# Attention over a paged cache: the products of a sequence's own values, for two sequences at once, as 64-row products in the two halves of the array

## The chip, the core and the metric

The kernel runs on one core of a Trainium2 chip. The metric is the device time of one execution in microseconds (us), as the median of several runs. The profile is one further execution, recorded by the hardware profiler. Its engines are TensorE (PE, with its weight loads listed apart as PEld), VectorE (DVE), ScalarE (ACT), GpSimd (POOL) and SyncE (SP).

## The reference, cut to what matters

Four residual layers are chained over x of 64 sequences x 32 tokens x 512 features, all in float32. The change touches only the third, an attention with a paged key-value cache:

```python
q = einsum('bsd,ed->bse', x, Wq).reshape(64, 32, 32, 128)      # 32 query heads
k = einsum('bsd,ed->bse', x, Wk).reshape(64, 32, 8, 128)       # 8 key heads
v = einsum('bsd,ed->bse', x, Wv).reshape(64, 32, 8, 128)
q, k = rope(rmsnorm(q)), rope(rmsnorm(k))
k_all = concatenate([k_cache[block_table], k], axis=1)         # 512 cached + 32 own keys
v_all = concatenate([v_cache[block_table], v], axis=1)
probs = softmax(where(valid, einsum('bqhd,bkhd->bhqk', q, k_all) * SCALE, -1e30))
o = einsum('bhqk,bkhd->bqhd', probs, v_all)
y = einsum('bse,de->bsd', o.reshape(64, 32, 4096), Wo)
```

Four query heads share one key head. For a sequence and a key head, the output is a sum over 512 cached values and over the sequence's own 32 values. The change concerns the second part.

## The kernel before, in words

The attention stage takes the 8 key heads in two halves of 4 (HKP = 4), and in each half the 16 tiles of 128 tokens (4 sequences of 32 tokens). That makes 32 steps. A step has 16 turns: 4 sequences b times 4 key heads g. The 128 rows of a turn are 4 query heads x 32 tokens.

The order on TensorE is written by hand: every matmul goes through `on_pe`, which chains it to the one before. A turn issues (loop from L831): `turned` (four 128x128 transposes of the turn's probabilities into `prT_ps`), a slot list, `start(i + 2)` (the scores of two turns ahead, two matmuls into `sc`), a second slot list, and `values` (four matmuls: 512 cached values against the turned probabilities, into `po`). The slot lists hold the projections of the next step (`pv`, `pk`, `pq`), the output product of the step before (`py`) and the transposes of the rotated queries and keys (`qkT_ps`). The order on the other engines is left to a scheduler that works when the program is built.

In the last turn of a sequence (g = 3) `own_turned` (L681) transposes the sequence's own probabilities. The result `own_prT` has 128 rows: 4 key heads x 32 own keys. `own_values` (L535) lays the own values out as `own_vt`, 128 rows x 4 slots x 128: the 32 rows of key head g are filled in slot g alone, and everything else is zero. So `own_part` (L696) can contract over all 128 rows for each g, in four 128x128x128 matmuls that add to the four groups of `po`, after which one DVE copy moves `po` (128x512, one PSUM bank) to `oT`. There are two `po` buffers, used by turns, and two each of `own_pr` and `own_vt`; `own_prT` has one.

In a float32 program each matmul stands in the trace as two passes, each with its own weight load, so the 4 matmuls are 8 records. A transpose is one record.

The evacuation, as it stands before:

```python
po = pos.pop(b)
for g in range(HKP):
    part(po[:, g, :], [(own_vts[b % 2][:, g, :], own_prT)], False, g == HKP - 1)
nc.vector.tensor_copy(oT[:, :, b % SEQ * S:(b % SEQ + 1) * S],
                      po.rearrange("p g (h s) -> p (g h) s", h=REP))
```

The first layer of the same kernel, which the change does not touch, multiplies 32 tokens of each of 4 sequences with weights of their own: at L183 four matmuls have 32 output partitions each and write the four quarters of one bank's partitions. The trace calls these `py<-w,xT 128*32`. The prediction reads them.

Of the kernel before, what the change touches and what calls it, by code (L numbers as in the profile page):

```python
# [24 lines left out]
F32 = mybir.dt.float32  # L25
# [8 lines left out]
P = 128  # L34
B, S, D = 64, 32, 512
NT = B * S // P
SEQ = P // S
# [6 lines left out]
HQ, HK, HD = 32, 8, 128  # L44
# [3 lines left out]
HKP = HK // HALVES  # L48
HQP = HQ // HALVES
REP = HQ // HK  # L50
# [410 lines left out]
def attention(c, known, x_in, y_part, y_out, tail):  # L461
# [10 lines left out]
    tc, nc, a = c.tc, c.nc, c.a  # L472
    half = HD // 2
    n_c = L // P
    with ExitStack() as outer:
        wvk = outer.enter_context(tc.tile_pool(name="l2_key_value_weights", bufs=1))
        xp = outer.enter_context(tc.tile_pool(name="l2_x", bufs=1))
        wk = outer.enter_context(tc.tile_pool(name="l2_work", bufs=1))
        kp = outer.enter_context(tc.tile_pool(name="l2_fixed", bufs=1))
# [5 lines left out]
        ps = ctx.enter_context(tc.tile_pool(name="l2_psum", bufs=1, space=PSUM))  # L485
# [8 lines left out]
        prs = [kp.tile([P, NK], F32, name=f"pr{i}") for i in range(3)]  # L494
        own_prs = [kp.tile([P, HKP * S], F32, name=f"own_pr{i}") for i in range(2)]
        vts = [kp.tile([P, n_c, HKP * HD], F32, name=f"vt{i}") for i in range(2)]
        own_vts = [kp.tile([P, HKP, HD], F32, name=f"own_vt{i}") for i in range(2)]
        for t in own_vts:
            nc.gpsimd.memset(t, 0.0)

        def transposes(tag, name, pieces):
            pt = ps.tile([P, len(pieces), P], F32, tag=tag, name=name)
            for m, piece in enumerate(pieces):
                c.on_pe(nc.tensor.transpose(pt[:, m, :], piece, c.ident))  # L504
            return pt

        def part(out, pairs, first, last):
            for i, (lhsT, rhs) in enumerate(pairs):
                c.on_pe(nc.tensor.matmul(out, lhsT, rhs, start=first and i == 0,  # L509
                                         stop=last and i == len(pairs) - 1))  # L510
# [24 lines left out]
        def own_values(b, v):  # L535
            j = b % SEQ
            for g in range(HKP):
                nc.vector.tensor_copy(own_vts[b % 2][g * S:(g + 1) * S, g, :],
                                      v[j * S:(j + 1) * S, g * HD:(g + 1) * HD])


# [138 lines left out]

        def own_turned(b):  # L681
            pt = transposes("tq", "own_prT_ps", [own_prs[b % 2]])
            own_prT = wk.tile([P, P], F32, name="own_prT")
            nc.scalar.copy(own_prT, pt[:, 0, :])
            return own_prT

        pos = {}

        def values(b, g, prT):

            if g == 0:
                pos[b] = ps.tile([P, HKP, P], F32, tag="po", bufs=2, name="po")
            part(pos[b][:, g, :], [(vts[b % 2][:, n, g * HD:(g + 1) * HD], prT[:, n, :])
                                   for n in range(n_c)], g == 0, False)

        def own_part(b, own_prT, oT):  # L696

            po = pos.pop(b)
            for g in range(HKP):
                part(po[:, g, :], [(own_vts[b % 2][:, g, :], own_prT)], False, g == HKP - 1)  # L700
            nc.vector.tensor_copy(oT[:, :, b % SEQ * S:(b % SEQ + 1) * S],  # L701
                                  po.rearrange("p g (h s) -> p (g h) s", h=REP))

        def weights(h, what):

# [46 lines left out]
        oTs, stores = {0: qp.tile([P, HQP, P], F32, name="oT")}, []  # L752
        p = projections[0]
# [36 lines left out]
        for s, (h, T) in enumerate(steps):  # L790
            if s:
                oTs[s] = qp.tile([P, HQP, P], F32, name="oT")
            slots = [[] for _ in range(2 * per)]
            if s == 0:
                slots[0].append(partial(projections[0].turned, 2))
                slots[2].append(partial(projections[0].turned, 3))
                slots[2].append(partial(own_keys, 0, 1, projections[0].kT))
            if s + 1 < len(steps):
                p = projections[s + 1]
                for what, at in zip(("v", "k") + GROUPS,  # L800
                                    ((1, 2), (3, 4), (6, 7), (8, 10), (11, 13), (14, 16))):
                    for u in range(2):
                        slots[at[u]].append(partial(p.product, what, u))
                for what, at in zip(("k",) + GROUPS, (9, 12, 15, 17, 20)):
                    slots[at].append(partial(p.turned, what))
            else:
                slots[16].append(tail.scaled)
                for m, at in enumerate((20, 22, 24, 26)):
                    slots[at].append(partial(tail.fold, ps, m))
            if s + 2 < len(steps):  # L810
                slots[18].append(projections[s + 2].load)
                slots[24].append(projections[s + 2].tables)
                slots[28].append(projections[s + 2].x)
                if steps[s + 2][0] != h:

                    for what, at in zip(("v", "k") + GROUPS, (3, 5, 8, 11, 14, 17)):
                        slots[at].append(partial(weights, steps[s + 2][0], what))
            if s + 2 == len(steps):
                for at, f in zip((17, 20, 23, 26, 29), tail.weights(wp, wvk)):
                    slots[at].append(f)  # L820
            if s:
                out = Output(*steps[s - 1], oTs.pop(s - 1), ws)
                for u, at in enumerate((18, 19, 21, 23, 25, 27, 29, 31)):
                    slots[at].append(partial(out.product, u))
                if steps[s - 1][0] != h:
# [357 lines left out]
```

## Time and profile before

| what | value |
|---|---|
| median of 3 runs (range) | 3809.74 us (3806.65 to 3811.78) |
| time of the profiled execution | 3798.88 us |
| span of the profiled execution | 3797.0 us |
| mean granted TensorE clock | 0.997 |
| PE / DVE / ACT / POOL busy | 3732.0 / 1797.3 / 1299.0 / 1284.4 us |
| attention stage, about 1173 to 3626 us of the span | PE busy 2446.5 of 2453.0 us |
| records of the own values' products on PE | 1024, 275 ns each |

The span runs from the first to the last instruction; the profiled execution took 1.9 us more than its span, and lies 10.9 us below the median of the runs. "Busy" is the union of the records of an engine, so matmuls that overlap are counted once. A record of a matmul reaches from its start to the end of its way through the array; records that follow each other overlap, so the spacing of their starts is what one costs the engine.

### The profile page before, as it was taken

What the parts mean: (1) busy time and instruction counts of PE and PEld (TensorE: products, weight loads), DVE (VectorE), ACT (ScalarE), POOL (GpSimd) and SP (SyncE); (2) the same over time, 40 slices, a digit from 0 to 9 for tenths busy, and PEclk for the clock granted to TensorE, in tenths of its full rate; (3) what the DMA queues carried; (4) which work ended last, traced back from release to release, by engine and by line L of the source; (5) the groups of instructions that cost most, each with busy time, mean ns of one, the idle gap of its engine ahead of it and who ended that gap; (6) DMA issues with size and microseconds to landing.
All of it is one profiled execution on the core that took longest, in us unless ns stands there. A gap on an engine that the chain in (4) does not pass through costs nothing.

```text
span 3797.0 us, 60480 instructions
## 1 busy us (share of the span) xinstructions
PE 3732.0 (98%) x17992; PEld 2629.6 (69%) x17992; DVE 1797.3 (47%) x4863; ACT 1299.0 (34%) x3008; POOL 1284.4 (34%) x1289
## 2 busy tenths in 40 slices
PE   6999999999999999999999999999999999999999
PEld 2444788888886777777777777777777777777755
DVE  5443111111116566555655565556555665556433
ACT  0111111111114444444444444444444444444411
POOL 0112100000006454444444444444444554444222
PEclk9999999999999999999999999999999999999999
DMA  5104211111115433444334346454444444444522
GB/s 191 34 26 165 89 42 42 42 42 45 35 55 164 130 115 115 118 120 117 114 117 122 115 155 197 145 151 119 118 121 125 118 118 121 122 123 117 156 69 62
DMA packets 402036, 407.45 MB, mean 107 GB/s; under 512 B 48592, under 2 KB 312784, under 8 KB 401712
## 3 DMA queue, kind: packets, MB, share of 16 engines
q1 hardware_dynamic: 352560, 241.68, 20.9%
q0 software_dynamic: 46848, 157.72, 13.7%
q10 hardware_dynamic: 2304, 4.20, 0.3%
q8 instruction: 147, 2.41, 0.3%
q14 instruction: 177, 1.45, 0.1%
HBM read 382.44 MB, written 20.97 MB: 106 GB/s over the span
## 4 chain that ended last, share of the span: by engine, by line
PE 94%; DVE 1%; issue 1%; ACT 1%; SPq 1%; DVEq 1%; DMA 1%; POOL 1%; POOLq 0%; ACTq 0%
PE po L509 15%; PE sc L660 12%; PE py L509 12%; PE pq L509 11%; PE prT_ps L504 6%; PE pg L122 5%; PE pu L122 5%; PE pz L122 4%; PE po L958 3%; PE ph L122 3%; PE pv L509 3%; PE pk L509 3%; PE pd L228 2%; PE qkT_ps L504 2%; PE pt L122 2%; PE py L183 1%
## 5 line engine op out<-in xcount | busy, mean ns | idle before, releaser
L531 POOL DMA_INDIRECT vt<-in_v_rows,v_rows x512 | 499.4, 975 | 823.7 <-PE po L509 727.7
L509 PEld LDWEIGHTS po<-prT,vt 128*128 128x128 f32 x4096 | 530.5, 192 | 183.1 <-issue 177.5
L665 DVE CUSTOM_DVE_ANT_0 pr<-sc,mask 128x544 f32<-128x544 f32 x512 | 369.1, 721 | 434.5 <-PE sc L660 433.9
L660 PE MATMUL sc<-kt,qT 128*128 128x288 f32 (+1 forms) x2048 | 556.1, 394 | 7.3 <-DMA kt<-in_kT 4.1
L667 ACT ACTIVATE pr<-pr,low 128x544 f32<-128x544 f32 x512 | 383.2, 748 | 501.9 <-DVE low L665 499.8
L509 PE MATMUL po<-prT,vt 128*128 128x128 f32 x4096 | 541.7, 275 | 0.0
L660 PEld LDWEIGHTS sc<-kt,qT 128*128 128x128 f32 x2048 | 369.4, 191 | 183.9 <-issue 108.7
L509 PE MATMUL py<-wo,oT 128*128 128x512 f32 x1024 | 480.2, 592 | 0.8 <-DVE oT L701 0.8
L509 PE MATMUL pq<-wq,xT 128*128 128x512 f32 x1024 | 480.7, 593 | 0.0
L678 ACT COPY prT<-prT_ps 128x512 f32<-128x512 f32 x512 | 299.4, 585 | 417.5 <-PE prT_ps L504 413.3
L672 DVE TENSOR_SCALAR pr<-pr,low 128x512 f32<-128x512 f32 x512 | 312.6, 611 | 16.7
L504 PE MATMUL prT_ps<-ident,pr 128*128 128x128 f32 x2048 | 307.7, 273 | 0.3 <-DVE pr L672 0.3
L509 PEld LDWEIGHTS py<-wo,oT 128*128 128x128 f32 x1024 | 191.9, 190 | 137.9 <-issue 125.8
L509 PEld LDWEIGHTS pq<-wq,xT 128*128 128x128 f32 x1024 | 182.4, 190 | 130.1 <-issue 125.3
L669 DVE RECIPROCAL low<-low 128x1 f32<-128x1 f32 x512 | 83.1, 162 | 347.8 <-ACT pr L667 346.7
L504 PEld LDWEIGHTS prT_ps<-ident,pr 128*128 128x128 f32 x2048 | 241.4, 142 | 0.4 <-issue 0.4
L126 POOL TENSOR_TENSOR rs<-rs,minus_half 128x4 f32<-128x4 f32 x160 | 166.4, 1040 | 196.3 <-DVE rs L547 195.1
L563 POOL TENSOR_TENSOR rot<-rot,swapped 128x512 f32<-128x512 f32 x160 | 202.8, 1267 | 1.0
L670 ACT ACTIVATE own_pr<-pr,low 128x32 f32<-128x32 f32 x512 | 164.1, 321 | 113.4 <-DVE low L669 113.4
L546 DVE TENSOR_REDUCE rs<-squares 128x4 f32<-128x512 f32 x160 | 109.6, 685 | 168.4 <-ACT squares L544 164.4
L564 POOL TENSOR_TENSOR rot<-rot,rs 128x512 f32<-128x512 f32 x160 | 177.7, 1110 | 8.0
L122 PE MATMUL pg<-xT,gate1T 128*128 128x256 f32 (+1 forms) x704 | 170.2, 382 | 0.8 <-DVE sg L334 0.8
(217 smaller groups left out, 4815.4 us busy)
## 6 DMA issues: line engine op xcount, KB each, us to landing
kt<-in_kT SPq DMA_DIRECT2D x2048, 64.0 KB
xt<-x SPq DMA_DIRECT2D x48, 256.0 KB
wq<-in_WqT SPq DMA_DIRECT2D x12, 1024.0 KB
sets<-in_cond0T SPq DMA_DIRECT2D x4, 2048.0 KB
vt<-in_v_rows,v_rows POOLq DMA_INDIRECT x512, 3.7
wo<-in_WoT SPq DMA_DIRECT2D x8, 1024.0 KB
y<-y SPq DMA_DIRECT2D x32, 256.0 KB
xT<-in_xT SPq DMA_DIRECT2D x4, 1024.0 KB
```

Of the source, the lines that this page charges most:

```text
L122: self.nc.tensor.matmul(out, lhsT, rhs, start=i == 0, stop=i == len(pairs) - 1)
L126: self.nc.gpsimd.tensor_tensor(t, t, self.minus_half[:, :n], ALU.pow)
L504: c.on_pe(nc.tensor.transpose(pt[:, m, :], piece, c.ident))
L509: c.on_pe(nc.tensor.matmul(out, lhsT, rhs, start=first and i == 0, stop=last and i == len(pairs) - 1))
L531: nc.gpsimd.indirect_dma_start(out=vts[b % 2][:, n, :], out_offset=None, in_=a["v_rows"], in_offset=bass.IndirectOffsetOnAxis(ap=rows[h][: ...
L563: nc.gpsimd.tensor_tensor(r, r, tmp, ALU.add)
L564: last = nc.gpsimd.tensor_tensor(r, r, rs.unsqueeze(2).to_broadcast([P, REP, HD]), ALU.mult)
L660: c.on_pe(nc.tensor.matmul(sc[:, lo + n * PSIZE:lo + m * PSIZE].rearrange("p (n k) -> p n k", k=PSIZE), q, kt[:, n:m, g, :], start=True, s ...
L665: nc.vector.tensor_tensor_reduce(pr[:, :NK], sc[:, lo:lo + NK], masks[h, b], -SCALE, 3.0e38, ALU.add, ALU.min, low[:, 0:1])
L667: nc.scalar.activation(pr[:, :NK], pr[:, :NK], AF.Exp, bias=low[:, 0:1], scale=-1.0, accum_out=low[:, 1:2])
L672: nc.vector.tensor_scalar(pr[:, :L], pr[:, :L], low[:, 2:3], None, ALU.mult)
L678: nc.scalar.copy(prT, pt)
```

## The change

The own values of two sequences (even b, then odd b) are multiplied together, after the odd one's last turn. `own_vt` shrinks to 2 slots: the rows of key heads 0 and 1 (rows 0 to 63) use slots 0 and 1, and so do those of key heads 2 and 3 (rows 64 to 127). A product is now taken over 64 rows. It is placed in the upper or the lower half of the array's rows, and the two halves write different PSUM banks: `po0` collects key heads 0 and 1 of both sequences, `po1` key heads 2 and 3. Each bank therefore lives through two sequences, and there is one buffer of each where there were two of `po`. The 8 own products of the two sequences are issued alternating between the halves. `own_prT` has two buffers, as the even sequence's is kept until the odd one's is there. Two DVE copies, one for each bank, move the results of both sequences. The own values of both sequences are laid out by calls in turns 0 and 2 of the even sequence, where each sequence's were laid out in the first turn of the sequence before it.

```diff
-        own_vts = [kp.tile([P, HKP, HD], F32, name=f"own_vt{i}") for i in range(2)]
+        own_vts = [kp.tile([P, 2, HD], F32, name=f"own_vt{i}") for i in range(2)]
...
-                nc.vector.tensor_copy(own_vts[b % 2][g * S:(g + 1) * S, g, :],
+                nc.vector.tensor_copy(own_vts[b % 2][g * S:(g + 1) * S, g % 2, :],
                                       v[j * S:(j + 1) * S, g * HD:(g + 1) * HD])
...
-            own_prT = wk.tile([P, P], F32, name="own_prT")
+            own_prT = wk.tile([P, P], F32, name="own_prT", bufs=2)
...
-            if g == 0:
-                pos[b] = ps.tile([P, HKP, P], F32, tag="po", bufs=2, name="po")
-            part(pos[b][:, g, :], [(vts[b % 2][:, n, g * HD:(g + 1) * HD], prT[:, n, :])
-                                   for n in range(n_c)], g == 0, False)
+            if b % 2 == 0 and g == 0:
+                pos[:] = [ps.tile([P, 2, 2, P], F32, tag=f"po{n}", name="po") for n in range(2)]
+            part(pos[g // 2][:, b % 2, g % 2, :], [(vts[b % 2][:, n, g * HD:(g + 1) * HD], prT[:, n, :])
+                                                   for n in range(n_c)], b % 2 == 0 and g % 2 == 0, False)
...
-        def own_part(b, own_prT, oT):
-            po = pos.pop(b)
-            for g in range(HKP):
-                part(po[:, g, :], [(own_vts[b % 2][:, g, :], own_prT)], False, g == HKP - 1)
-            nc.vector.tensor_copy(oT[:, :, b % SEQ * S:(b % SEQ + 1) * S],
-                                  po.rearrange("p g (h s) -> p (g h) s", h=REP))
+        def own_part(b, own_prTs, oT):
+            for u in range(2):
+                for g in range(2):
+                    for n in range(2):
+                        q = slice(n * P // 2, (n + 1) * P // 2)
+                        part(pos[n][:, u, g, :], [(own_vts[u][q, g, :], own_prTs[u][q, :])],
+                             False, u == g == 1)
+            at = (b - 1) % SEQ * S
+            for n in range(2):
+                nc.vector.tensor_copy(
+                    oT[:, 2 * n * REP:2 * (n + 1) * REP, at:at + 2 * S]
+                    .rearrange("p m (u s) -> p m u s", u=2),
+                    pos[n].rearrange("p u g (h s) -> p (g h) u s", h=REP))
...
                 if g == HKP - 1:
-                    own_prT = own_turned(b)
+                    own_prTs = ([] if b % 2 == 0 else own_prTs) + [own_turned(b)]
...
-                if g == HKP - 1:
-                    own_part(b, own_prT, oTs[s])
-                elif g == 0 and i:
-                    own_values_of(i + HKP)
+                if b % 2 and g == HKP - 1:
+                    own_part(b, own_prTs, oTs[s])
+                elif b % 2 == 0 and g in (0, 2) and i >= HKP:
+                    own_values_of(i - g + g // 2 * HKP)
```

More of the change, by code (lines that the diff above doesn't have):

```diff
@@ L682, in own_turned @@
             pt = transposes("tq", "own_prT_ps", [own_prs[b % 2]])
-            own_prT = wk.tile([P, P], F32, name="own_prT")
+            own_prT = wk.tile([P, P], F32, name="own_prT", bufs=2)
             nc.scalar.copy(own_prT, pt[:, 0, :])
             return own_prT
-        pos = {}
+        pos = []
         def values(b, g, prT):
-            if g == 0:
-                pos[b] = ps.tile([P, HKP, P], F32, tag="po", bufs=2, name="po")
-            part(pos[b][:, g, :], [(vts[b % 2][:, n, g * HD:(g + 1) * HD], prT[:, n, :])
-                                   for n in range(n_c)], g == 0, False)
-        def own_part(b, own_prT, oT):
-            po = pos.pop(b)
-            for g in range(HKP):
-                part(po[:, g, :], [(own_vts[b % 2][:, g, :], own_prT)], False, g == HKP - 1)
-            nc.vector.tensor_copy(oT[:, :, b % SEQ * S:(b % SEQ + 1) * S],
-                                  po.rearrange("p g (h s) -> p (g h) s", h=REP))
+            if b % 2 == 0 and g == 0:
[15 more added lines that the diff above has]
+                    pos[n].rearrange("p u g (h s) -> p (g h) u s", h=REP))
         def weights(h, what):
```

## The prediction

> **What bounds the kernel now.** I read the page first, then the groups of instructions by shape, the waits of TensorE inside the attention stage, and the timeline around the own products and around the first layer's narrow matmuls.
>
> ```profile
> span 3797.0 us, 60480 instructions
> PE 3732.0 (98%) x17992; PEld 2629.6 (69%) x17992; DVE 1797.3 (47%) x4863; ACT 1299.0 (34%) x3008; POOL 1284.4 (34%) x1289
> ...
> PEclk9999999999999999999999999999999999999999
> ...
> PE 94%; DVE 1%; issue 1%; ACT 1%; SPq 1%; DVEq 1%; DMA 1%; POOL 1%; POOLq 0%; ACTq 0%
> PE po L509 15%; PE sc L660 12%; PE py L509 12%; PE pq L509 11%; PE prT_ps L504 6%; PE pg L122 5%; PE pu L122 5%; PE pz L122 4%; PE po L958 3%; PE ph L122 3%; PE pv L509 3%; PE pk L509 3%; PE pd L228 2%; PE qkT_ps L504 2%; PE pt L122 2%; PE py L183 1%
> ```
>
> TensorE is busy 98% of the span at full clock, and 94% of the chain that ended last lies on it. The waits of PE between 1200 and 3610 us are these, in total us, times and the longest:
>
> ```profile
> PE sc L660 <- DMA kt<-in_kT: 4.1, 3, 3.0
> PE sc L660 <- DVE low L665: 0.8, 1, 0.8
> PE qkT_ps L504 <- POOL rot L564: 0.6, 1, 0.6
> PE prT_ps L504 <- DVE pr L672: 0.3, 1, 0.3
> ```
>
> That is 5.8 us in 2410. So PE time taken out of this stage comes out of the end, and new PE time goes onto it, until another engine is late. DVE is 47% busy. These are the groups the change touches:
>
> ```profile
> L538 DVE COPY own_vt<-v 32x128 f32<-32x128 f32 x512 | 137.5, 269 | 51.8 <-PE po L509 42.2 <-issue 2.3
> L509 PE MATMUL po<-own_prT,own_vt 128*128 128x128 f32 x1024 | 135.3, 275 | 0.0
> ...
> L701 DVE COPY oT<-po 128x512 f32<-128x512 f32 x128 | 87.8, 686 | 3.1 <-PE po L509 2.3
> ```
>
> The 135.3 us is the union of records with their tails. The cost is the spacing of starts, which the timeline shows (start, duration, engine, count):
>
> ```profile
> 2411.06 0.97 PEld L509 LDWEIGHTS po<-own_prT,own_vt 128*128 128x128 f32 x8
> ...
> 2411.17 1.06 PE L509 MATMUL po<-own_prT,own_vt 128*128 128x128 f32 x8
> ...
> 2412.06 0.60 PE L504 MATMUL prT_ps<-ident,pr 128*128 128x128 f32 x4
> ```
>
> From 2411.17 to 2412.06, 8 passes take 0.89 us: 0.112 us each, the loads at the same spacing hidden behind them. Two sequences cost 1.79 us, all 64 pairs 114 us.
>
> **The change: what the products cost.** There are 8 products of 64 rows for a pair, so still 16 passes and 16 loads; only running two at once can gain. No row of the trace has 64x128 products. The nearest is L183, where four matmuls use quarters of the array's columns:
>
> ```profile
> 80.38 3.70 PE L122 MATMUL ph<-yT,up 128*128 128x512 f32 x8
> ...
> 84.01 0.16 PEld L183 LDWEIGHTS py<-w,xT 128*32 128x32 f32 x8 [0.76 <-issue]
> ...
> 84.01 1.92 PE L183 MATMUL py<-w,xT 128*32 128x512 f32 x16
> 85.87 3.70 PE L122 MATMUL ph<-yT,up 128*128 128x512 f32 x8
> ```
>
> A full-array pass of 512 columns starts every 0.43 us. Sixteen one after another would take 6.9 us; these took 1.92, so four run at once. The two passes of each matmul do not prevent it.
>
> From 80.38 to 85.87 are 5.49 us; 8 full passes and 4 quartets at 0.428 make 5.14. So going into the split array and back costs 0.35 us: each time the array runs empty and the next load lies open. Here the load on the way in has 32 columns. Ours has 128, and the load rows below say 192 against 111 ns, 0.08 more: **0.43 us for a pair's two switches**.
>
> If two halves run at once, a pair takes 8 slots of 0.112, 0.89 us, plus 0.43: 1.32 against 1.79, saving 0.46, times 64 **29.6 us**.
>
> **Two rules of the Trainium skill, against the rows.** The section "LDWEIGHTS (loading the stationary operand)" of "TensorE: Matmul & The Clock Gate" speaks against the change: a load's time follows its columns, not its rows.
>
> ```profile
> L509 PEld LDWEIGHTS po<-own_prT,own_vt 128*128 128x128 f32 x1024 | 124.6, 192 | 0.0
> ...
> L183 PEld LDWEIGHTS py<-w,xT 128*32 128x32 f32 x512 | 20.8, 111 | 73.3 <-DVE w L179 41.9 <-issue 29.0 <-DVE coeffs L878 0.8
> ...
> L122 PEld LDWEIGHTS pz<-actT,down1T 96*128 96x128 f32 x64 | 12.2, 191 | 1.7
> ```
>
> The trace agrees: 96 rows load in 191 ns as 128 do in 192. Halving the rows shortens no load, and loads already come every 0.112 us. If they pass one by one, 16 take 1.79 us, and the sum becomes plus 0.43 x 64 = 27.5 us. Against that stands the load row at 84.01: eight loads of 111 ns each within 0.16 us. By the slope (81 ns for 96 columns) 32 columns take 0.027 us, so eight in a row would end at 0.30. Loads into different parts of the array do overlap, at least when the parts are columns. The section "Key Properties" of "TensorEngine Tiling (Array Packing)" says it for parts in general, and also that a change of mode drains the array, by an amount it doesn't name; the 0.35 us is that amount here. No run yet shows row halves. Ends: minus 29.6 and plus 27.5. I take the first, since the nearest row shows both matmuls and loads at once.
>
> **What is moved and who could be late.** The order of instructions in the changed kernel leaves PE as it was but for these products; ACT, POOL and SP keep their instructions, the vt and kt DMAs among them, so no queue is passed. `own_prT`'s second buffer is copied turns earlier; the odd one's copy (271 ns on ACT) stands ahead of its products as before, so it costs nothing.
>
> The new wait: each bank has one buffer, so the next pair's first `values` waits for po0's copy on DVE. The built order puts six `own_vt` copies ahead of the two oT copies, and these wait for the pair's products. The same place before, at a step's start:
>
> ```profile
> 2391.30 0.85 DVE L538 COPY own_vt<-v 32x128 f32<-32x128 f32 x3
> ...
> 2392.16 0.69 DVE L701 COPY oT<-po 128x512 f32<-128x512 f32 x1
> ...
> 2394.84 1.05 PE L509 MATMUL po<-prT,vt 128*128 128x128 f32 x8
> ```
>
> The own products started at 2390.88, the next values 3.96 later. After, with 1.32 in place of 0.89, the values start at 4.39. On DVE the first `own_vt` copy can go at about 0.74 (0.2 for the switch, 0.22 for a product, its tail and the 0.15 that the copy started late before); six at 0.22 end at 2.06, the first oT copy at 2.75, the second at 3.4. Slack 1.6 us. In mid-step a reciprocal (0.16) and a scaling (0.49 to 1.1) stand between, so 3.4 to 4.0, but the values come at 4.8: a query projection (1.72) and transposes (0.44) lie ahead. Slack 0.8 to 1.4. Only the last step has no projection to cover this: its values come at 2.7, waiting some 1 us in all, and the last output product waits for one copy more, 0.7. Together **2 us**. Were the cover gone everywhere, it would be up to 1.3 us x 64 = 83 us.
>
> DVE's copies number 128 and 512 as before. They stand denser, so the scores' first DVE step (L665) after a pair comes about 1.4 us later at a step's start and 0.7 in mid-step; the transposes that need it are two turns, over 5 us, off. The last rotated query of a step reaches its transposes 1.26 us early now. Its DVE part moves about half a us, and PE there comes 0.43 later: covered.
>
> Sum: minus 29.6 plus 2 is minus 27.6. Profiled: 3798.9 to 3771.3. That execution lies 10.9 below the median; all the change is on PE, so I take it from the median: 3809.7 - 27.6 = **3782 us**.
>
> **Rivals.**
> - *Loads of the two halves queue up* (slower). Place: the own block; price 27.5 us: 3837. It decides from where overlap saves less than 0.43 of the 0.89 us, about half. For it: the load's length doesn't fall with rows, and it is as long as the pass. Against: L183. 11%.
> - *Passes keep program order over the halves.* A product's two passes share a half, so only the second of one meets the first of the next: 9 slots instead of 8, 0.112 x 64 = 7 us less: 3789. Speaking against it, 16 narrow passes fit four slots at L183. 9%.
> - *Switches cost less*, their two open loads (0.11 each) hidden: 0.24 a pair, 12 us more gain: 3770. 6%.
> - *The single banks bind.* If DVE is later than reckoned by more than the slack, each 0.3 us at each pair is 19 us: 3801; at 0.45 the gain is gone. For it: one buffer in place of two, and DVE's scheduled order. Against: 47% busy. 8%.
> - *The change doesn't do what it says*: in the built program the products are set to rows 0 and 64 of the array, so I put this under the first rival.
>
> **How the numbers follow.** Two at once with both switches: 66%, 3782, its own range 3774 to 3790. The range 3768 to 3803 takes in the second and third rival and the mild half of the fourth, about 85%; it leaves out queued loads. A measurement here can tell about 0.2%, 8 us, from no change. Faster: 66 + 9 + 6 + 2 = 83%; same: 4%; slower: 11 + 2 = 13%.
>
> **What would show it.** Right: 16 own passes in about 1.0 us of starts, in pairs a few ns apart; transposes starting about 1.3 us after the first; PE busy down by nearly 30 us; no new PE wait on L708 but in the last step. Wrong: own loads one by one every 0.11 us (first rival); pairs offset by a pass (second); PE `po` waiting on DVE `oT` dozens of times (fourth).

## The result, and the profile after

| | before | after | ratio (95% interval) |
|---|---|---|---|
| median of 6 runs (range), us | 3809.68 (3806.28 to 3812.89) | 3797.27 (3793.71 to 3803.30) | 0.9969 (0.9957 to 0.9982) |
| profiled execution / its span, us | 3798.88 / 3797.0 | 3800.24 / 3798.5 | |

The change gains 12.4 us where 27.6 were predicted. In the two traces even less is seen of it: from the first turn of the attention stage to its last one the kernel before takes 2439.3 us and the kernel after 2435.5, which is 3.8 us less. The page of the kernel after says:

```profile
span 3798.5 us, 60417 instructions
PE 3705.5 (98%) x17992; PEld 2581.5 (68%) x17992; DVE 1787.7 (47%) x4863; ACT 1287.6 (34%) x3008; POOL 1289.5 (34%) x1289
```

PE is busy 26.5 us less (3732.0 before), yet the span did not shrink. So the products became cheaper and TensorE stands still instead. The groups of the products, by shape (busy us, mean ns of one, idle time before):

```profile
L509 PE MATMUL po<-own_prT,own_vt 64*128 64x128 f32 x1024 | 74.4, 285 | 0.0
L509 PEld LDWEIGHTS po<-own_prT,own_vt 64*128 64x128 f32 x1024 | 62.1, 187 | 7.7
L538 DVE COPY own_vt<-v 32x128 f32<-32x128 f32 x512 | 125.9, 246 | 53.9 <-PE po L509 37.1 <-issue 4.5 <-PE prT_ps L504 0.8
L708 DVE COPY oT<-po 128x512 f32<-128x512 f32 x128 | 82.8, 686 | 8.5 <-remote 2.2 <-PE po L509 1.3 <-PE sc L660 1.3
```

A load of 64 rows lasts as long as one of 128 did (187 against 192 ns), but the union of the loads halves, from 124.6 to 62.1 us: two lie beside each other. Where TensorE stands still is in its waits between 1200 and 3610 us, the same stretch as before:

```profile
PE po L509 <- ACT prT L678: 15.0, 7, 3.4
PE sc L660 <- DMA kt<-in_kT: 7.0, 4, 2.5
PE po L509 <- issue: 5.3, 16, 2.1
PE sc L660 <- DVE low L665: 2.3, 2, 1.3
PE qkT_ps L504 <- POOL rot L564: 0.5, 1, 0.5
```

The first line is new: the values' products wait for `prT`, ScalarE's copy of the turned probabilities. ScalarE is 34% busy, so the question is what that copy waits for. The waits of ACT in this stretch:

```profile
ACT prT L678 <- PE prT_ps L504: 270.7, 292, 3.0
ACT prT L678 <- PE sc L660: 113.5, 41, 4.3
ACT prT L678 <- remote: 31.8, 7, 5.8
```

Before, there was one such line (prT_ps, 408.5 us, 368 times). The copy reads only the four transposes. Yet 41 times it starts only when the scores, issued behind them, have ended as well. One such place, at the start of a step (start, duration; idle time before and what ended it):

```profile
1548.59 0.97 PEld L509 LDWEIGHTS po<-own_prT,own_vt 64*128 64x128 f32 x16
1548.59 1.16 PE L509 MATMUL po<-own_prT,own_vt 64*128 64x128 f32 x16
1549.12 1.63 DVE L538 COPY own_vt<-v 32x128 f32<-32x128 f32 x6 [0.22 <-issue]
...
1549.68 0.66 PE L504 MATMUL prT_ps<-ident,pr 128*128 128x128 f32 x4
...
1550.18 1.08 PE L660 MATMUL sc<-kt,qT 128*128 128x288 f32 x4
...
1550.78 1.29 DVE L708 COPY oT<-po 128x512 f32<-128x512 f32 x2
...
1551.10 1.88 PE L509 MATMUL pv<-wv,xT 128*128 128x512 f32 x4
...
1552.60 0.58 ACT L678 COPY prT<-prT_ps 128x512 f32<-128x512 f32 x1 [4.35 <-PE sc L660]
...
1553.24 1.16 PE L509 MATMUL po<-prT,vt 128*128 128x128 f32 x8 [0.26 <-issue]
1554.05 0.72 DVE L665 CUSTOM_DVE_ANT_0 pr<-sc,mask 128x544 f32<-128x544 f32 x1 [1.52 <-remote]
```

The transposes end at 1550.34 and ScalarE has been idle since 1548.25, but the copy starts at 1552.60, 2.26 us late, and the values start at once when it is done. VectorE's first step on the scores (L665, the last line) is late as well: the scores ended at 1551.26, and it starts at 1554.05.

An instruction announces its end by counting up a semaphore on which the other engines wait, and the trace records these counts with their times. One of TensorE's stands 23 ns before the copy and one 23 ns before VectorE's step, the first 1.3 us and the second 2.8 us after the scores, the last instruction before them that announces anything. So it is TensorE's announcement that comes late, to whichever engine waits for it, and not ScalarE that is slow. Of the 124 `prT` copies of this trace that are over 0.5 us late, 67 start within 25 ns of such a record; at the others none stands, for some records are missing (see the third batch).

Below, the time from the end of a turn's fourth transpose to the start of its `prT` copy is "the lag". In the trace of before its median is at most 0.21 us in each of the 16 turns of a step. After, in the first turn of a step (turn 0, which follows the products of the second pair of the step before), it is 2.20 us in the median and up to 3.74.

### The profile page after: what moved, and what is told of

Its sections match the earlier page's. It is cut to its first block, busy times and chain, and to the rows that moved or that the text cites. A ratio compares the mean times of both kernels' runs of the same rounds, so it can differ in the third digit from the quotient of the medians.

```text
span 3798.5 us, 60417 instructions
## 1 busy us (share of the span) xinstructions
PE 3705.5 (98%) x17992; PEld 2581.5 (68%) x17992; DVE 1787.7 (47%) x4863; ACT 1287.6 (34%) x3008; POOL 1289.5 (34%) x1289
## 3 DMA queue, kind: packets, MB, share of 16 engines
q14 instruction: 178, 1.45, 0.1%
## 4 chain that ended last, share of the span: by engine, by line
PE 92%; SPq 2%; issue 1%; ACT 1%; DVE 1%; DVEq 1%; another core or an unknown queue 1%; DMA 1%; POOL 0%; ACTq 0%; POOLq 0%
PE po L509 13%; PE sc L660 12%; PE pq L509 12%; PE py L509 11%; PE prT_ps L504 6%; PE pg L122 5%; PE pu L122 5%; PE pz L122 4%; PE po L967 3%; PE ph L122 3%; PE pk L509 3%; PE pv L509 3%; PE pd L228 3%; PE qkT_ps L504 2%; PE pt L122 2%
## 5 line engine op out<-in xcount | busy, mean ns | idle before, releaser
L665 DVE CUSTOM_DVE_ANT_0 pr<-sc,mask 128x544 f32<-128x544 f32 x512 | 368.7, 720 | 472.2 <-PE sc L660 394.4
L672 DVE TENSOR_SCALAR pr<-pr,low 128x512 f32<-128x512 f32 x512 | 324.8, 634 | 16.8
L122 PE MATMUL pu<-xT,up1T 128*128 128x256 f32 (+1 forms) x704 | 166.3, 379 | 0.0
```

The lines of the kernel that those rows point to most:

```text
L122: self.nc.tensor.matmul(out, lhsT, rhs, start=i == 0, stop=i == len(pairs) - 1)
L665: nc.vector.tensor_tensor_reduce(pr[:, :NK], sc[:, lo:lo + NK], masks[h, b], -SCALE, 3.0e38, ALU.add, ALU.min, low[:, 0:1])
L672: nc.vector.tensor_scalar(pr[:, :L], pr[:, :L], low[:, 2:3], None, ALU.mult)
```

## Experiments

Eighteen runs, of the two kernels and of nine variants, were made in five batches, each batch on a chip of its own, with the kernel before beside it. No chip was met twice. The four theories that the expectations name are: (1) the own products announce their end eight times a pair (in the trace 506 of the 512 matmuls carry an announcement of their own), and many announcements in a short time hold up TensorE's later ones; (2) the split array does it; (3) the copies on VectorE do it, dense as they are, with the oT copies last; (4) SyncE's bursts of page-number reads do it, 35 register reads with checks in some 7 us in every fourth turn.

### First batch

**e1_before_again**: the kernel before, unchanged.

> The kernel before, unchanged, for a second trace of it. In its first trace ScalarE's copy of prT starts within 0.25 us of the end of the four transposes in all turns, while in the changed kernel it starts 0.8 to 3.7 us late in the first turn after a pair's own products. Theory A (late completions are brought by the change): again no such lateness here, time 3799 to 3813. Theory B (it is chance of a run): some lateness of over 0.5 us here too.

3808.6 us, beside 3808.05 (median of 16). Here even the kernel before has late copies: 0.90 us in the median in turn 9, 0.04 in turn 0. TensorE waits 1.5 us for `prT` in the stretch. So a slighter lateness is there without the change.

**e2_pair_full**: the kernel after, with products over all 128 rows (own_vt with 4 slots again; one buffer less for y makes the room).

```diff
-                        part(pos[n][:, u, g, :], [(own_vts[u][q, g, :], own_prTs[u][q, :])],
+                        part(pos[n][:, u, g, :], [(own_vts[u][:, 2 * n + g, :], own_prTs[u])],
```

> The changed kernel with its own products over all 128 rows again (own_vt back at 4 slots with zeros), still issued for two sequences at once into the two banks, each product still announcing its end to a semaphore; y_before shares the y buffer to make room. Theory 1 (announcements of many products in a short time hold up TensorE's later ones): they now come singly every 0.22 us instead of in pairs, so less lateness or none; own block 1.79 us a pair; no gain of PE time; 3806 to 3815. Theory 2 (the split array itself holds up announcements): no lateness, 3806 to 3813. Theory 3 (one buffer per bank and the dense VectorE copies make PE wait): the first values of a step wait as in the changed kernel, about 19 us in all: 3825 to 3832.

3813.49 us, ratio 1.0017 (1.0008 to 1.0025). Without the split array the pairing loses 5.4 us. In the traced execution (3824.08 us, 10.6 above the median) TensorE waits:

```profile
PE po L509 <- ACT prT L678: 13.5, 7, 2.9
```

The lag in turn 0 is 0.21 us in the median, up to 3.16. So theory 2 is not the whole: late copies come with the pairing alone, though fewer (9 of 32 first turns at 0.9 us or more; e1 has 3, at 1.1).

**e3_after_nobounds**: the kernel after, without SyncE's checks of the page numbers.

```diff
-                src, engines=[mybir.EngineType.SP], min_val=0, max_val=n - 1)
+                src, engines=[mybir.EngineType.SP], min_val=0, max_val=n - 1,
+                skip_runtime_bounds_check_because="page numbers are drawn below PAGES")
```

> The changed kernel without the bounds checks on the page numbers that SyncE reads, so with 9169 minus 4109 SyncE instructions. SyncE's burst of such instructions lies beside the own products in turns 7 and 15, and it pauses for 0.5 to 0.7 us where TensorE's completions come late. Theory 4 (SyncE's burst and TensorE's announcements hold each other up): lateness gone or shorter, 3775 to 3788. Theories 1, 2, 3: unchanged, 3793 to 3803.

3776.80 us, ratio 0.9919 (0.9902 to 0.9935). Lag in turn 0 1.44 us in the median, in turn 13 0.04 (after: 1.01).

**e4_oT_first**: the kernel after, with each `own_vt` copy put behind the last oT copies in VectorE's order. A pair's products then announce twice, not eight times, since the first announcement that is needed is that of a whole bank.

```diff
+                if moved:
+                    tc.add_manual_dep(
+                        ins.ins, moved[-1],
+                        mybir.DependencyInfo(mybir.DependencyClass.NoSync, mybir.DependencyReason.DATA),
+                        reason="own values after the banks are moved")
```

> The changed kernel with VectorE's copies of own_vt ordered behind the two oT copies, so that a pair's 8 own products announce their ends 2 times instead of 8, and po0 is free six copies (1.3 us) sooner. Theory 1 (many announcements): the lateness after own products goes, and with it the 19 us of PE waits in the first turn of a step: 3776 to 3784. Theory 2 (split array itself): lateness stays, 3793 to 3803. Theory 3 (bank freed late): waits go but the late prT copies stay: 3778 to 3786. Theory 4: lateness stays, 3793 to 3803.

3783.44 us, ratio 0.9934 (0.9918 to 0.9951). Lag in turn 0 0.69 us in the median.

Both lie well below the kernel after of the result, e3 by 20.5 us and e4 by 13.8. But the kernel after had not run in this batch, so neither had a control.

### Second batch

**e5_before_nobounds**: e3's edit on the kernel before.

> The kernel before with SyncE's checks of the page numbers left out (the numbers themselves are the same). It says how much of the time of e3 was only the checks and no matter of the change. The trace of before shows about 5.8 us of waits of TensorE in the attention stage. If the checks cost time only where the change has used up the slack (theories 1 and 4), this kernel takes 3800 to 3808 us, and the change without checks is worth about 25 to 30 us, near the 27.6 us that were predicted. If the checks cost 20 us in any kernel (their own path, or what comes before and after the attention stage), it takes about 3785 to 3790, and the change without checks is worth only about 12 us.

3798.90 us beside 3803.43, ratio 0.9988 (0.9981 to 0.9994). The checks alone are worth 4.5 us. The traces show where, beside e16, the kernel before on another chip of this kind: TensorE waits 2.4 us in all for keys (`kt`) here and 6.4 there, nearly all of it in the last step, and behind such waits the granted clock falls to 0.5, for 3.4 us here and for 6.8 there. At half clock half of the time is lost, so that makes 4.0 + 1.7 us, and the stage is 5.7 us shorter.

**e6_both**: e3 and e4 together.

> The kernel after with both: no checks of page numbers on SyncE, and the own_vt copies behind the two oT copies on VectorE. e3 and e4 recovered about 20 and 16 us one by one. If both act on the same loss (theory 4: TensorE's announcements and SyncE's burst of register reads hold each other up, so that taking away either is enough), this kernel takes about 3772 to 3778 us, no more than a few us below e3. If they act on separate losses (theory 1 for the announcements, and the checks costing time by themselves), the gains add up: about 3760 us. Waits of values for ScalarE's prT copy: under 5 us in all by both.

3765.85 us, ratio 0.9898 (0.9882 to 0.9915); lag in turn 0 0.04 us, and TensorE waits 0.3 us in all for `prT`. Which theory this speaks for can only be said with e8.

**e7_own_vt_pool**: the `own_vt` copies on GpSimd.

```diff
-                nc.vector.tensor_copy(own_vts[b % 2][g * S:(g + 1) * S, g % 2, :],
+                nc.gpsimd.tensor_copy(own_vts[b % 2][g * S:(g + 1) * S, g % 2, :],
```

> The kernel after with the own_vt copies on GpSimd instead of VectorE. The two oT copies are then first on VectorE after a pair's products, as in e4, but the own products still announce six times a pair (e4: twice, after: eight times). Theory 1 (many announcements in a short time hold up the later ones): the transposes of the first turn of a step are still announced 1 us or more late in the median, the values wait 10 us or more for prT in all, and the time stays near 3795 us. Theory 3 (the dense copies on VectorE, the oT copies last): the lateness falls to a few tenths in the median as nothing dense is left on VectorE, and the time is about 3780 us, as in e4. If GpSimd with these copies becomes late for the rotated queries, TensorE waits on POOL at the query transposes (L504), and the time says nothing on either.

3966.27 us, ratio 1.0430 (1.0413 to 1.0447). TensorE's waits (between 1200 and 3700 us, as the stage is longer) and the group of the moved copies say why:

```profile
PE qkT_ps L504 <- POOL rot L564: 138.0, 31, 7.1
```

```profile
L538 POOL COPY own_vt<-v 32x128 f32<-32x128 f32 x512 | 163.7, 320 | 173.2 <-DMA vt<-in_v_rows,v_rows 122.3 <-PE sc L660 29.0 <-PE pv L509 3.3
```

GpSimd stands 122 us ahead of these copies for loads of values, and what is queued behind, the rotated queries, comes up to 7.1 us late. As the expectation said for this case, it tells nothing of the lateness.

**e8_after_again**: the kernel after, unchanged.

> The kernel after once more, unchanged, for a second trace: how much of the late announcements and of the waits for prT repeats. If they come from the program (theories 1 to 4), the first turn of nearly every step is again late by 1 to 3 us in the median, and values wait for prT 10 to 20 us in all. If they were an accident of one execution, the lag is under 0.2 us in most steps and the time is near 3782 us.

**3770.7 us**, 32.7 below the 3803.43 of before, in a single execution. The lag in turn 0 is 0.04 us, never above 0.08. Nothing of the loss that the experiments were to explain is there. So what e6 gained on this chip over the kernel after (4.9 us) is about what the checks cost by themselves (4.5), and e6 tells nothing of lateness.

### Third batch: is it the chip?

**e9_after_timed**: the kernel after, timed.

> The kernel after, timed against the kernel before on one chip. e8 took 3770.7 us beside 3803.4 of before on its chip and showed no late prT copies in a step's first turn, while the result measured 3797.3 beside 3809.7, with the copies late by 2.2 us in the median. Two readings: (a) the lateness belongs to the chip that a run lands on: on a chip that shows it the gain is 10 to 17 us and the first turn's lag 1 to 3 us, on one that doesn't the gain is 30 to 34 us and the lag under 0.1, nothing in between, and the before kernel reads about 3808 on the former and about 3803 on the latter. (b) e8 was one lucky execution: on any chip the runs of this kernel scatter between 3765 and 3800.

3798.32 us (13 runs, 3792.86 to 3803.44) beside 3808.16, ratio 0.9973 (0.9965 to 0.9982). The lag in turn 0 is 2.22 us in the median. Its waits are those of the result:

```profile
PE po L509 <- ACT prT L678: 17.6, 8, 3.5
PE po L509 <- issue: 5.2, 16, 1.7
PE sc L660 <- DMA kt<-in_kT: 2.6, 3, 1.8
```

The lag takes few values: of the 32 first turns, 2 are at 0.04 to 0.08 us, 9 at about 0.8, 15 at 2.2 and 6 at 3.7. Steps with the second value lose nothing, those with the third about 0.5 us, those with the last about 2.0. In 26 of the 32 steps the value is the one that the trace of the result has. The values lie about 1.45 us apart, and so do TensorE's recorded counts at the place shown above (1551.11, 1552.58 and 1554.03).

**e10_both_again**: the kernel of e6.

> The kernel after without SyncE's checks and with the own_vt copies behind the oT copies, once more, beside the kernel after on the same chip. On a chip with late announcements: about 3765 to 3772 us, 25 us or more below the kernel after, since both changes lessen the lateness. On a chip without: within about 8 us below the kernel after, since e8 lost almost nothing that they could give back; what remains is the last step (e8 +0.5 us, e6 -0.8) and the checks' own 4.5 us seen in e5.

3776.20 us, ratio 0.9916 (0.9901 to 0.9931): 22 us below the kernel after on the same chip, and as fast as e3 was with one of the two edits. In the first turns of steps 1 to 30 e9 loses 17.3 us against a trace without lateness (e13, below), e3 6.3, e11 6.9 and e10 2.0. The two edits win back 11.0 and 10.4 us one by one (e3 on another chip than e9) and 15.3 together, so in part they act on the same loss.

**e11_oT_first_again**: the kernel of e4.

> The kernel after with the own_vt copies behind the two oT copies on VectorE. If its gain in e4 (3783.4 beside 3797.3 of after, which ran on another day or chip) was the chip and not the order, it is equal to the kernel after here within 3 us. If the order of the copies lessens the lateness (theories 1 and 3), it is 10 us or more below the kernel after on a chip that shows lateness, and equal to it on one that doesn't.

3787.92 us, ratio 0.9942 (0.9927 to 0.9957), 10.4 below the kernel after; turn 0 lies 0.76 us late in the median. The order of VectorE's copies, with the fewer announcements, does act on such a chip; which of these two it is was not told apart.

**e12_static_pages**: the kernel after with fixed pages, so that SyncE reads no page numbers.

```diff
-            pages = c.numbers(a["pages"][0:1, b * NPP:(b + 1) * NPP], PAGES)
             for n in range(NPP):
-                c.load_by(kts[h, b][:, n, :], a["kT"][ds(pages[n], 1), h].rearrange("a d f -> (a d) f"))
+                c.load_by(kts[h, b][:, n, :], a["kT"][(b * NPP + n) % PAGES, h])
```

> The kernel after with the page numbers of the key loads fixed in the program: SyncE reads no page numbers, so its bursts of register reads with checks (35 reads, about 7 us, in every fourth turn) are gone; the DMAs move as many bytes, from other pages. This part of the computation is left out. Theory 4 (the bursts hold up TensorE's announcements): on a chip with lateness, every lag after a pair's products falls below 0.1 us in the median and the time is about 3770 us. Theory 1 (the announcements among themselves): the lag of the first turn stays at 1 us or more there, and the time is no better than e3's 3777. On a chip without lateness: about the kernel after less the 4.5 us of e5.

3769.89 us, ratio 0.9900 (0.9884 to 0.9915), 28.4 below the kernel after. PE's and ACT's waits:

```profile
PE po L509 <- issue: 4.7, 8, 2.0
...
PE po L509 <- ACT prT L677: 0.7, 2, 0.5
```

```profile
ACT prT L677 <- PE prT_ps L504: 351.7, 339, 2.9
ACT prT L677 <- PE sc L659: 28.6, 9, 4.3
```

TensorE's waits for `prT` go from 17.6 to 0.7 us. The time is what theory 4 said, but the lag was to fall below 0.1 us and stays at 0.78 in turn 0. That is less than the slack of about 1.9 us (below), so it costs almost nothing. Taking SyncE's reads away brings the lag from 2.2 to 0.8; something is left, for which theory 1 remains. Not all of the 28.4 us is lateness: the waits for keys (2.6 us in e9) are gone too. Turn by turn, 15.0 us of the gain lie in the first turns of steps 1 to 30.

### Fourth and fifth batch: the controls

**e13_after_timed2**: the kernel after once more.

> The kernel after, timed once more. By the reading that lateness belongs to the chip: on a chip where before reads about 3803, the kernel after takes 3768 to 3774 us (ratio about 0.991) and its first-turn lag is under 0.1 us in the median; on one where before reads about 3808 it takes 3793 to 3803 and the lag is 2.2 us. By the reading of a lucky execution: about 3797 on either, with single runs near 3770.

3773.00 us beside 3802.57, ratio **0.9919 (0.9905 to 0.9932)**, a gain of 29.6 us. Lag in turn 0 0.04 us. The same place of the program as above, on this chip:

```profile
1542.98 1.16 PE L509 MATMUL po<-own_prT,own_vt 64*128 64x128 f32 x16
1543.50 1.64 DVE L538 COPY own_vt<-v 32x128 f32<-32x128 f32 x6 [0.22 <-PE po L509]
...
1544.07 0.66 PE L504 MATMUL prT_ps<-ident,pr 128*128 128x128 f32 x4
...
1544.76 0.58 ACT L678 COPY prT<-prT_ps 128x512 f32<-128x512 f32 x1 [2.13 <-PE prT_ps L504]
...
1545.17 1.29 DVE L708 COPY oT<-po 128x512 f32<-128x512 f32 x2
...
1546.95 0.72 DVE L665 CUSTOM_DVE_ANT_0 pr<-sc,mask 128x544 f32<-128x544 f32 x1
...
1547.20 1.05 PE L509 MATMUL po<-prT,vt 128*128 128x128 f32 x8
```

From the products' start, the `own_vt` copies (0.52), the transposes (1.09) and the oT copies (2.19) are where they are in the trace of the result to 0.01 us. What moved are the two that wait for TensorE's later announcements: the `prT` copy, 1.78 here and 4.01 there, and VectorE's step on the scores, 3.97 here and 5.46 there. The values come at 4.22 here, at 4.65 there. The copy here ends at 2.36, so the values have 1.86 us of slack over it; a lag of 2.2 us takes that and some 0.4 more, one of 3.7 some 1.9 more, as e9's steps show. ACT's and PE's waits of e13:

```profile
ACT prT L678 <- PE prT_ps L504: 350.4, 370, 2.5
ACT prT L678 <- ACT pr L667: 0.3, 1, 0.3
```

```profile
PE sc L660 <- DMA kt<-in_kT: 7.1, 5, 4.7
PE sc L660 <- DVE low L665: 1.6, 2, 1.3
PE po L509 <- issue: 1.4, 2, 1.1
```

**e14_static_oT_first**: fixed pages and e4's order.

> The kernel after with fixed page numbers (SyncE reads none; this part of the computation is left out) and the own_vt copies behind the oT copies, so that a pair's own products announce twice and not eight times. If the bursts of SyncE and the dense announcements are the two sources of the lateness, the first turn's lag is under 0.1 us in the median on any chip, TensorE's waits for prT are under 1 us, and the time is 3762 to 3768 us. If the lag stays near 0.7 us, as in e4, e10, e11 and e12, there is a third source that none of these runs touched, such as the products in halves by themselves.

3759.11 us, ratio 0.9883 (0.9867 to 0.9898), lag 0.04 us. But e13 shows that this chip has no lateness with the plain kernel either, so the question it was made for got no answer.

**e15_before_static**: fixed pages without the change.

> The kernel before with fixed page numbers (SyncE reads none; this part of the computation is left out). If SyncE's reads cost the kernel before nothing but what e5 showed (4.5 us), it takes 4 to 8 us less than before; the change itself is then worth 28 to 34 us where no pages are read (e12 took 3769.9 beside 3808.2). If it takes 20 us or more off, e12's gain was mostly the reads and not the lateness behind the change.

3794.43 us, ratio 0.9978 (0.9969 to 0.9987). Fixed pages alone are worth 8.1 us here. TensorE has no wait for keys left in the stretch and the stage no time at half clock, where e16, on the same chip, has 6.4 us of waits and 6.8 us at half clock. That is 6.4 + 3.4 of the 10.0 us by which the stage is shorter. So what the reads cost the kernel before is that keys come late to a few turns, nearly all in the last step. Of e12's 28.4 us over the kernel after, some 20 are therefore the lateness, with the reservation that the two ran on different chips.

**e16_before_trace**: the kernel before, for its trace beside e13.

> The kernel before, unchanged, for its trace on this chip. On a chip with lateness: the lag of the prT copy is about 0.9 us in a step's turn 9, as in e1, and near zero in turn 0, and TensorE waits for prT 1 to 2 us in all. On one without: no turn later than 0.25 us in the median, as in the first trace of before.

3804.2 us; no turn is later than 0.21 us in the median. With it the change can be read turn by turn on one chip: the attention stage takes 2441.7 us before and 2409.0 after (e13), 32.7 less.

**e17_static_oT_first** and **e18_after_third**:

> The kernel of e14 once more: fixed page numbers (SyncE reads none; this part of the computation is left out) and the own_vt copies behind the oT copies. If this chip shows lateness (e18 tells it by its first-turn lag), a lag under 0.1 us in turn 0 says that the two sources are all; one of 0.5 us or more says that something else is left. On a chip without lateness it repeats e14's 43 us below before and leaves this open.

> The kernel after on the same chip as e17. First-turn lag 2.2 us in the median and a time about 10 us below before on a chip with lateness; 0.04 us and about 30 us below before on one without.

3760.57 us, ratio 0.9882 (0.9866 to 0.9899), and 3774.22 us, ratio 0.9919 (0.9902 to 0.9935), beside 3804.29. This chip too is without lateness (0.04 us in e18), so e17 leaves open what e14 left open.

The kernel after on all chips on which it was timed:

| batch | before, us | after, us | gain, us | lag in turn 0, median us |
|---|---|---|---|---|
| result | 3809.68 | 3797.27 | 12.4 | 2.20 |
| third (e9) | 3808.16 | 3798.32 | 9.8 | 2.22 |
| second (e8, one run) | 3803.43 | 3770.70 | 32.7 | 0.04 |
| fourth (e13) | 3802.57 | 3773.00 | 29.6 | 0.04 |
| fifth (e18) | 3804.29 | 3774.22 | 30.1 | 0.04 |

There are two kinds of chip and nothing between, as far as these five tell; since none was met twice, a lasting property of the chip and a state of it at that hour are not told apart. The traces differ in a second way. Of the 3594 instructions of TensorE that count up its semaphore, 3372 counts are recorded in the result's trace and 3365 in e9's, but 3580, 3584 and 3578 in those of e8, e13 and e18. Of the 3470 of the kernel before, 3288 are recorded in e1's trace, 3468 in e16's, and 3465 in the first trace of before. Whether a missing count was not recorded or came together with another, the trace does not tell. On the first batch's chip the kernel after did not run; its before (3808.05) and its lags are of the first kind. Each kind repeats within 4 us.

The fastest version with all of the computation in it is that of e6 and e10, faster than both kernels on either kind of chip: 3765.85 us where before took 3803.43, and 3776.20 where before took 3808.16. It rests on page numbers that are known to be valid.

## Why the prediction was right and wrong

**The products: right, and slightly better.** The starts of a pair's 16 passes come in twos, 7 ns apart, with 0.112 us from one two to the next, on both kinds of chip. From the first to the next transposes it takes 1.09 us. The way in costs 0.09 more than the 0.112 between passes of before, the second slot starts 0.1 late, the way out costs 0.1, and the next turn begins 0.06 later: about 0.35 us for both switches, as at L183. The 0.08 added for a load of 128 columns was not there. A pair saves 0.545 us instead of 0.46, and 64 pairs 34.9 us instead of 29.6. e13 beside e16 shows it turn by turn: 0.89 us less in each turn in which an even sequence ends, 0.29 more in each with an odd one's end, 0.06 more in the turn behind it. The first two rivals fell with this; the third, cheaper switches, came true by half (0.35 lies between 0.43 and its 0.24; 0.43 less two loads of 0.11 would be 0.21). The rule that a load's time follows its columns holds (187 ns for 64 rows), and did not decide: loads into two row halves overlap, as the section "Key Properties" of "TensorEngine Tiling (Array Packing)" in the Trainium skill says for parts in general.

**VectorE's timeline: right.** Six `own_vt` copies were to end 2.06 us after the first product; they end at 2.16. The oT copies were to end at 2.75 and 3.4; the second ends at 3.48. The values were to start at 4.39 and start at 4.22. PE's `po` waits for an oT copy in the last step alone: the two waits of 0.3 and 1.1 us that e13's lines put down to "issue" end 0.1 us after the first oT copy of the pair, and "some 1 us in all" had been predicted. So the rival of the single banks fell; that its 3801 us lies nearest to the result is chance. The 0.7 us for one copy more before the last output product was not there: it waits 0.8 us for `oT` in e13, but in e16 too.

**The step that failed is "who could be late".** Its sum of 2 us held only waits for VectorE's copies. ScalarE was put at nothing because it "keeps its instructions", and the slack of its `prT` copy over the values (1.86 us) was not worked out. On the chips of the result's kind TensorE's announcement of the transposes comes later than that: the traced wait of the values for `prT`, put at 0, is 15.0 us in the result, with 5.3 us beside it that the lines put down to "issue", most of it in the first turns of a step. Between e13 and e9, turn by turn, the stage loses 27.0 us: 17.3 in the first turns of a step, 1.2 in turn 9, 3.4 in the second-last turns, which are not waits for `prT` but longer waits for keys (1.6 us) and 3.4 us at half clock behind one of them, and 5.0 in the first and the last step. Between the kinds the kernel before loses only 4.0 us (2445.7 us in e1 against 2441.7 in e16); its late copies are fewer (45 over 0.5 us in e1, 119 in e9) and at most 1.64 us late. The difference, 23 us, against the 17 to 20 that the table shows between the gains of the two kinds where both were timed in rounds, is what the prediction had no term for.

**The step from the trace to the median was the second fault.** The profiled execution of before lay 10.9 us below the runs, and the prediction took the gain off the median as if the 10.9 were an offset without a bearing on the change. At 3798.9 us, with lags of at most 0.21 us, that trace looks like the chips without lateness (3802.6 to 3804.3) and not like those of the runs (3808 to 3810), and its 3465 recorded counts say the same. On which chip it was taken is not known. On chips without lateness the 27.6 us predicted lie inside the measured interval: e13's is 25.9 to 36.1 us. In part that is luck, as the products alone saved 5.3 us more than predicted; the stage keeps 32.7 us of their 34.9, and the medians show 29.6.

**What causes the lateness** is shown only in part. On a chip that has it, it goes down with SyncE's page reads taken away (e12: waits for `prT` 17.6 to 0.7 us), with their checks left out (e3, on another chip; waits for `prT` still 12.2 us), and with VectorE's order changed and fewer announcements (e11: 10.4 us). e10 shows that the last two act in part on one loss. In the full array (e2) it is there as well. Theory 3 and theory 1 were not separated. In the Trainium skill, "The cost: per-tile semaphore tail" of "TensorE: Matmul & The Clock Gate" says that announcements of concurrent products go one after another, about 26 ns each, and advises one for all. Eight of them would make 0.21 us, an estimate from that page. In e13 the recorded announcements of two products that end 7 ns apart stand 42 or 43 ns apart, so by the trace it is more, 0.34 us for eight. The traces show no loss at all on one kind of chip (0.04 us) and 2.2 to 3.7 us on the other, so neither figure gives what was found. Why chips differ, and by which way reads on SyncE delay announcements of TensorE, stays open. So does whether anything is left when both sources are away: e14 and e17 met only chips without lateness.

## What to carry to other kernels

When a trace and the timed runs differ by more than the runs do among themselves, ask first whether the trace shows the same machine: a slack read from it may not be there in the runs. Work out the slack of every hand-over that a shortened stretch of TensorE had covered, on the engines whose work does not change too, and set it against the latest announcement that any trace shows. That alone would not have been enough here: the latest `prT` copy in any trace of the kernel before is 1.64 us late (e1), the slack is 1.86, and the 2.2 to 3.7 us came with the change. A wait that ends with an instruction issued behind the one whose data are needed (here the copy of `prT`, released with the scores) points to a late announcement and not to a slow engine.

## What the runs showed of the hardware

- Two products of 64 rows in the two row halves of the array, writing two PSUM banks, run at once, loads included: from the first of 16 passes of 128 columns to the start of what follows it takes 1.09 us, where 16 over all rows take 1.79. Going into the halves and back costs about 0.35 us.
- On some chips the end of TensorE's transposes, 4 of them right behind a group of such products, reaches ScalarE 0.8, 2.2 or 3.7 us late and at few values between; on others the same program has at most 0.08 us there. VectorE is told late too: in e9 its step on the scores is more than 0.3 us behind e13's place in 27 of 32 first turns, and 10 of the 128 oT copies, which wait for the products themselves, are up to 2.6 us behind.
- 35 reads of page numbers with their checks on SyncE, in every fourth turn, are worth 4.5 us (checks) and 8.1 us (all) in the kernel before, by the traces as waits for keys (6.4 us in e16, 2.4 in e5, none in e15) and time at half clock behind them (6.8, 3.4 and 0 us), and some 20 us more in the kernel after on a chip with late announcements.
- A single wait of TensorE can be followed by a slower clock: behind one of 1.8 us (e9, step 15) the granted clock was 0.5 for 3.4 us, behind one of 4.7 us (e13, last step) for 6.8.
